# A small memset on GpSimd behind every gather of listed edges

## The chip, the core and the metric

The kernel runs on one core of a Trainium2 chip. Its time is the device time of one execution in microseconds (us). TensorE (PE in the profile, its weight loads PEld), VectorE (DVE), ScalarE (ACT), GpSimd (POOL) and SyncE (SP) each work through an instruction stream of their own, in order, and wait for one another through semaphores.

## What is computed

A graph network with 6250 nodes and 200000 edges: a layer norm with a ReLU, then three layers that take, for every node, the maximum over its incoming edges of the source nodes' rows, and put it through two linear maps. The input is added at the end. The destinations are drawn so that low-numbered nodes have many more edges than high-numbered ones. The widths of a node's row are 128, 256 and 256 on the way into the three layers, and 128 at the end.

```python
def _sage_conv(x, src, dst, Wl, bl, Wr):
    agg = jax.ops.segment_max(x[src], dst, num_segments=x.shape[0])
    agg = jnp.where(jnp.isfinite(agg), agg, 0.0)
    return agg @ Wl + bl + x @ Wr
...
h = jax.nn.leaky_relu(_sage_conv(h, src, dst, Wl1, bl1, Wr1), 0.01)   # and so for layers 2 and 3
...
h = jnp.maximum(_layernorm(x, axis=-1), 0.0)
x = x + _L0_gnn_ref(h, edge_index, ...)
```

## The kernel before

The 6250 nodes lie in 50 tiles of 127 nodes. A first part (to about 270 us in the profile) normalizes the rows and sorts the edges into units. Each unit is a tile of destinations; the edges that fit a regular pattern (one edge for each destination of the unit and each pair of source tiles) are taken by TensorE, the rest stand in lists and are gathered.

**The dense path.** A step is a layer, a group of units (four of them), a pair g of source tiles (25 of them) and a chunk of destinations of up to 512 (layers 1 and 2) or 1024 columns (layer 0). In `one_hots` (L916) a distance product on TensorE goes to PSUM (`sq`, L926, two buffers), and ScalarE turns it into a one-hot matrix (`hot`, L930, eight buffers). In `products` (L934) TensorE multiplies the pair's rows with it (`pg`, L943, two PSUM buffers), and in `maxima` (L948) VectorE takes the maximum with the accumulator `acc` (L955, L957). The loop over steps issues the one-hots of step t between the products of step t-1. There are 200 steps in layer 0 and 350 in each of the layers 1 and 2. SyncE loads the pair of a coming group of steps ahead (`load_pair`, L913, three buffers).

**The listed edges.** The class `Listed` (L959) does the rest. A list has a row of 128 x `len(units)` destinations and a depth for each unit (`CAPS`); one gather fetches, for one unit and one depth, 128 source rows from the layer's table in DRAM with an indirect DMA that GpSimd issues (L980), into a tile `g` of a ring with eight buffers. The indices come as int16 from `ell`; every six (layer 0) or four gathers, ScalarE copies the next ones to an int32 tile `let` (L979, eight buffers). `maximum` (L985 on) merges the tiles on VectorE (L994, L999), and SyncE writes the unit's result to `best` in DRAM (L1003). The depths sum to 145, 291 and 181 in the three lists: 617 gathers in a layer and 1851 in all.

**The finish of a unit.** `Node` (from L1006) fetches the list's result with another indirect DMA of GpSimd (L1025), transposes it on TensorE, merges it with `acc` on VectorE (L1047), runs the linear maps (L1052 to L1060) and writes the new row tables that the next layer gathers from (L1068 on, and L876 to L889). `Joined` does the same for destinations with very many edges (L1095).

**The order.** The scheduler doesn't reorder anything: each engine's stream is in the order of the code. A plan made by hand puts each gather, maximum and finish on a step's agenda (`plan`, `agenda`, `whens`). The gathers of a layer are spread evenly over its steps, ahead of the last of the group's steps that need them, and the maximum follows its gather by 8 steps in layer 0 and 6 in the others. On GpSimd the gathers thus stand in one queue with the fetches (L1025, L1095) and, in the first part and early in layer 0, with the sends of the lists' rows. A send (`send_row`, L599) is a memset of a 128x1 tile `gap_t` (L600) and an indirect DMA that scatters a row of indices to DRAM (L601). In the sends and the gathers alike, GpSimd's DMA_INDIRECT rows in the profile are the time in which it writes the transfer's descriptors, not that of the transfer itself.

A general path (another function) is there for inputs that don't fit the lists; it isn't run for these inputs.

Of the kernel before, what the change touches and what calls it, by code (L numbers as in the profile page):

```python
# [34 lines left out]
BF16 = mybir.dt.bfloat16  # L35
# [6 lines left out]
P = 128  # L42
# [21 lines left out]
def kernel(ctx: ExitStack, tc: tile.TileContext, x, src, dst,  # L64
                    Wl1, bl1, Wr1, Wl2, bl2, Wr2, Wl3, bl3, Wr3, out):
    nc = tc.nc
# [54 lines left out]
    node = main.enter_context(tc.tile_pool(name="node", bufs=1))  # L121
# [771 lines left out]
        nc.vector.memset(hT[:, :, R:], 0.0)  # L893


    RING = 8

    def chunks(layer, k):
# [60 lines left out]
    class Listed:  # L959
# [11 lines left out]
        def gather(self, t):  # L971
            q, j = self.seq[t]
            b, i = divmod(j, self.B)
            if i == 0:
                self.tiles[q, b] = ring.tile([P, self.B, self.F], F32, tag="g", name="g", bufs=RING)
            if j % self.n == 0:
                n = min(self.n, CAPS[self.k][q] - j)
                self.let = ring.tile([P, 6], I32, tag="let", name="let", bufs=8)
                nc.scalar.activation(self.let[:, :n], ell[self.k][:, q, j : j + n], AF.Identity, scale=1.0)  # L979
            nc.gpsimd.indirect_dma_start(  # L980
                out=self.tiles[q, b][:, i, :], out_offset=None, in_=tables[self.layer],
                in_offset=bass.IndirectOffsetOnAxis(ap=self.let[:, j % self.n : j % self.n + 1], axis=0),
            )

        def maximum(self, t):  # L985
            q, j = self.seq[t]
            b, i = divmod(j, self.B)
            m = CAPS[self.k][q]
            if i < self.B - 1 and j < m - 1:
                return  # L990
            base = self.tiles[q, 0]
            if b:
                g = self.tiles.pop((q, b))
                nc.vector.tensor_max(base[:, : i + 1, :], base[:, : i + 1, :], g[:, : i + 1, :])  # L994
            if j == m - 1:
                w = min(m, self.B)
                while w > 1:
                    h = w // 2
                    nc.vector.tensor_max(base[:, :h, :], base[:, :h, :], base[:, w - h : w, :])  # L999
                    w -= h  # L1000
                n = len(LISTS[self.k])
                view = self.to[: n * P, :].rearrange("(p q) f -> p q f", q=n)
                nc.sync.dma_start(view[:, q, :], base[:, 0, :])  # L1003
                del self.tiles[q, 0]
# [587 lines left out]
```

## Time and profile before

| | us |
|---|---|
| median of three runs | 4034.6 (4028.16 to 4065.68) |
| time of the profiled execution | 4023.28 |
| span of the profiled execution | 4021.5 |
| mean granted TensorE clock | 0.854 of full speed |
| busy: TensorE, its weight loads, VectorE, ScalarE, GpSimd | 2844.8, 1818.3, 2433.2, 1477.0, 2214.0 |
| GpSimd: 1851 gathers (L980) | 1868.4 busy |

In rows of groups of instructions, the engine and operation stand first, then the tiles written and read, the shapes and the count; behind the bar the busy time in us, the mean of one instruction in ns, then the idle time of the engine just before such instructions and what ended most of it. In rows of the timeline the start in us and the duration stand first; in brackets stands the engine's idle time before the instruction, with what released it: "issue" is an engine that waited for nothing the profile shows, "remote" a release that it can't place. In rows of stages the stretch is followed by its length, then by busy us and the number of instructions of each engine, the granted clock, the DMA engines' busy share and GB/s; where a row is restricted to a line or a tile, only the engines that it concerns stand in it.

### The profile page before, as it was taken

What the parts mean: (1) busy time and instruction counts of PE and PEld (TensorE: products, weight loads), DVE (VectorE), ACT (ScalarE), POOL (GpSimd) and SP (SyncE); (2) the same over time, 40 slices, a digit from 0 to 9 for tenths busy, and PEclk for the clock granted to TensorE, in tenths of its full rate; (3) what the DMA queues carried; (4) which work ended last, traced back from release to release, by engine and by line L of the source; (5) the groups of instructions that cost most, each with busy time, mean ns of one, the idle gap of its engine ahead of it and who ended that gap; (6) DMA issues with size and microseconds to landing.
All of it is one profiled execution on the core that took longest, in us unless ns stands there. A gap on an engine that the chain in (4) does not pass through costs nothing. (4 is left out here: it accounts for less than half of the span.)

```text
span 4021.5 us, 37441 instructions
## 1 busy us (share of the span) xinstructions
PE 2844.8 (71%) x10999; PEld 1818.3 (45%) x10999; DVE 2433.2 (61%) x3806; ACT 1477.0 (37%) x3139; POOL 2214.0 (55%) x2251
## 2 busy tenths in 40 slices
PE   1044586456644557888888788898888878788787
PEld 1022343233322334555555554565555545455455
DVE  5578576445523344555667677684565667667784
ACT  4322254233322235444433333344444433333233
POOL 5552556665566521566766566631566766567631
PEclk9997687677665679999998898999998988888888
DMA  8111123233322334444545454665344544444545
GB/s 258 38 31 32 40 64 65 72 96 92 91 64 67 102 100 146 121 129 130 121 149 158 149 166 133 198 186 186 110 133 124 121 126 143 123 131 124 175 144 162
DMA packets 261722, 482.67 MB, mean 120 GB/s; under 512 B 54993, under 2 KB 151877, under 8 KB 260867
## 3 DMA queue, kind: packets, MB, share of 16 engines
q0 software_dynamic: 93184, 233.28, 22.3%
q1 hardware_dynamic: 168259, 246.70, 19.0%
q8 instruction: 89, 1.46, 0.2%
q14 instruction: 126, 1.03, 0.1%
q10 hardware_dynamic: 64, 0.20, 0.0%
HBM read 389.65 MB, written 90.31 MB: 119 GB/s over the span
## 5 line engine op out<-in xcount | busy, mean ns | idle before, releaser
L980 POOL DMA_INDIRECT g<-table,let x1851 | 1868.4, 1009 | 1319.8 <-ACT let L979 601.2
L943 PE MATMUL pg<-hot,pair_sb 128*128 128x512 f32 x7000 | 2297.5, 467 | 377.3 <-DVE acc L957 234.7
L957 DVE TENSOR_TENSOR acc<-acc,pg 128x1024 f32<-128x1024 f32 (+3 forms) x1189 | 1379.0, 1172 | 1178.4 <-PE pg L943 447.6
L930 ACT ACTIVATE hot<-sq 128x512 fp32r<-128x512 f32 (+1 forms) x2100 | 1209.6, 590 | 2010.5 <-PE sq L926 1034.8
L943 PEld LDWEIGHTS pg<-hot,pair_sb 128*128 128x128 f32 x7000 | 1420.6, 211 | 970.3 <-issue 372.9
L926 PE MATMUL sq<-lookup,dist 77*128 77x512 bf16 (+1 forms) x1725 | 691.0, 420 | 329.1 <-issue 185.9
L926 PEld LDWEIGHTS <-dist 77*128 77x128 bf16 x2100 | 195.8, 104 | 711.4 <-issue 710.1
L994 DVE TENSOR_TENSOR g<-g 128x1024 f32<-128x1024 f32 (+5 forms) x285 | 297.2, 1043 | 5.4 <-DMA g<-table,let 5.0
L926 PE MATMUL sq<-lookup_o,dist 77*128 77x512 bf16 x375 | 156.6, 433 | 92.6 <-issue 54.1
L1025 POOL DMA_INDIRECT agg<-best,end_i x141 | 137.3, 974 | 99.1 <-PE aT_p L1041 60.7
L999 DVE TENSOR_TENSOR g<-g 128x512 f32<-128x512 f32 (+3 forms) x356 | 177.9, 500 | 10.6
L1054 PE MATMUL z_p<-wr,hT_in 128*128 128x256 f32 (+1 forms) x500 | 143.8, 406 | 0.0
L1060 ACT ACTIVATE s<-z_p,low,slope 128x256 f32<-128x256 f32 x100 | 56.5, 565 | 219.3 <-PE z_p L1056 108.8
L1056 PE MATMUL z_p<-wl,mz 128*128 128x256 f32 (+1 forms) x500 | 125.6, 369 | 1.2 <-DVE mz L1047 1.1
L1054 PEld LDWEIGHTS z_p<-wr,hT_in 128*128 128x128 f32 x500 | 83.2, 209 | 95.2 <-issue 82.0
L1047 DVE TENSOR_TENSOR mz<-acc,aT_p 128x256 f32<-128x256 f32 (+1 forms) x141 | 52.3, 371 | 111.7 <-PE aT_p L1041 46.3
L1095 POOL DMA_INDIRECT agg_v<-best,end_i x24 | 22.7, 948 | 162.4 <-PE vT_p L1104 76.0
L1056 PEld LDWEIGHTS z_p<-wl,mz 128*128 128x128 f32 x500 | 92.8, 211 | 12.9 <-DVE mz L1047 2.0
L1052 PE MATMUL z_p<-bias,ones_b 3*128 3x256 bf16 (+1 forms) x150 | 41.3, 275 | 72.3 <-DVE h L1068 52.5
L979 ACT ACTIVATE let<-ell 128x4 int32<-128x4 int16 (+5 forms) x475 | 92.0, 199 | 0.0
L601 POOL DMA_INDIRECT picks<-picked,to_i x55 | 58.7, 1068 | 38.5 <-DVE rank_h L577 28.7
L885 DVE TENSOR_TENSOR pr<-h,pr 128x256 fp32r<-128x256 f32 x100 | 42.4, 424 | 58.7 <-ACT pr L876 49.1
(281 smaller groups left out, 1195.8 us busy)
## 6 DMA issues: line engine op xcount, KB each, us to landing
pair_sb<-pair SPq DMA_DIRECT2D x200, 512.0 KB
g<-table,let POOLq DMA_INDIRECT x1851
pair_sb<-pair SPq DMA_DIRECT2D x100, 256.0 KB
pair<-pr SPq DMA_DIRECT2D x100, 256.0 KB
best<-g SPq DMA_DIRECT2D x110, 128.0 KB
table<-h SPq DMA_DIRECT2D x100, 128.0 KB
across<-hT SPq DMA_DIRECT2D x100, 128.0 KB
hT_in<-across SPq DMA_DIRECT2D x100, 128.0 KB
```

The source lines that it names most:

```text
L601: s = nc.gpsimd.indirect_dma_start(out=picks[k], out_offset=bass.IndirectOffsetOnAxis(ap=to_i[k][:, i : i + 1], axis=0), in_=picked[k][:, ...
L926: nc.tensor.matmul(d_p[:, :bw], dist[:, 2 * g + s, :], from_[:, base + b : base + b + bw], start=True, stop=True)
L930: nc.scalar.activation(hot[:, :bw], d_p[:, :bw], AF.Relu, bias=1.0, scale=-1.0)
L943: nc.tensor.matmul(to, pr[:, s, i, kk * P : (kk + 1) * P], hot[:, :bw], start=((alone or s == 0) and i == 0), stop=((alone or s == 1) and ...
L957: nc.vector.tensor_max(to, to, of)
L979: nc.scalar.activation(self.let[:, :n], ell[self.k][:, q, j : j + n], AF.Identity, scale=1.0)
L980: nc.gpsimd.indirect_dma_start(out=self.tiles[q, b][:, i, :], out_offset=None, in_=tables[self.layer], in_offset=bass.IndirectOffsetOnAxis ...
L994: nc.vector.tensor_max(base[:, : i + 1, :], base[:, : i + 1, :], g[:, : i + 1, :])
L999: nc.vector.tensor_max(base[:, :h, :], base[:, :h, :], base[:, w - h : w, :])
L1025: nc.gpsimd.indirect_dma_start(out=self.agg[:, : self.F], out_offset=None, in_=of, in_offset=bass.IndirectOffsetOnAxis(ap=at, axis=0),)
L1054: nc.tensor.matmul(z_p, self.hT[:, i, :], wr[layer][:, i, :], start=False, stop=False)
L1056: nc.tensor.matmul(z_p, self.m[:, i, :], wl[layer][:, i, :], start=False, stop=(i == K - 1))
```

## The change

A tile `pace_t` of 128 partitions with 400 bf16 elements each is allocated once, and behind each gather GpSimd fills it with zeros. Nothing else reads or writes the tile.

```diff
+    pace_t = node.tile([P, 400], BF16, name="pace_t")
     RING = 8
...
             nc.gpsimd.indirect_dma_start(
                 out=self.tiles[q, b][:, i, :], out_offset=None, in_=tables[self.layer],
                 in_offset=bass.IndirectOffsetOnAxis(ap=self.let[:, j % self.n : j % self.n + 1], axis=0),
             )
+            nc.gpsimd.memset(pace_t, 0.0)
```

In the built program GpSimd's stream has 1851 more instructions, one behind each L980; 1848 of them wait on GpSimd's own semaphore for the memset before, and none of the gathers has a new wait. The streams of the other engines are the same, instruction by instruction, with the same waits. Lines from L896 on move by one, those behind the gather by two.

## The prediction

> **What bounds the kernel now.** I read the page first (busy shares, slices, groups), then a table of busy times by stage, then the waits, and last the timeline around two chains of GpSimd transfers.
>
> ```profile
> span 4021.5 us, 37441 instructions
> PE 2844.8 (71%) x10999; PEld 1818.3 (45%) x10999; DVE 2433.2 (61%) x3806; ACT 1477.0 (37%) x3139; POOL 2214.0 (55%) x2251
> POOL 5552556665566521566766566631566766567631
> L980 POOL DMA_INDIRECT g<-table,let x1851 | 1868.4, 1009 | 1319.8 <-ACT let L979 601.2
> L930 ACT ACTIVATE hot<-sq 128x512 fp32r<-128x512 f32 (+1 forms) x2100 | 1209.6, 590 | 2010.5 <-PE sq L926 1034.8
> ```
>
> No engine is full over the span. POOL's slices show the gathers of each layer as a plateau of 5 to 7 tenths, with a low slice at the end of each layer. The stages must be read apart. In the next table each row is a stretch: its length, then busy us and instructions of PE, PEld, DVE, ACT and POOL, then TensorE's granted clock. The long rows are the gather phases of layers 0, 1 and 2; the 100 us rows are the ends of the same layers, where nothing is gathered.
>
> ```profile
> 468.00:1450.00 982.00, 545.07 (x1789) 320.89 (x1789) 457.92 (x849) 325.83 (x716) 590.10 (x613) 0.69 0.30 79
> 1500.00:1600.00 100.00, 78.05 (x310) 44.97 (x309) 45.16 (x71) 52.42 (x104) 12.28 (x13) 0.94 0.50 152
> 1663.00:2650.00 987.00, 836.16 (x3330) 549.04 (x3329) 665.18 (x721) 388.33 (x848) 645.45 (x634) 0.92 0.51 150
> 2700.00:2800.00 100.00, 89.89 (x399) 59.11 (x398) 53.82 (x53) 45.60 (x85) 10.42 (x11) 1.00 0.59 197
> 2860.00:3870.00 1010.00, 829.32 (x3321) 539.37 (x3320) 668.09 (x731) 362.83 (x788) 661.45 (x645) 0.89 0.47 134
> 3900.00:4000.00 100.00, 90.46 (x400) 59.27 (x401) 59.59 (x60) 42.21 (x78) 10.41 (x11) 0.98 0.59 183
> ```
>
> Without gathers PE issues 310, 399 and 400 matmuls per 100 us. At those rates the gather phases need 1789/3.10 = 577, 3330/3.99 = 835 and 3321/4.00 = 830 us, and they last 982, 987 and 1010. So 405, 152 and 180 us are lost in them, and no engine's own work explains it. The same view for the gathers' line alone (POOL busy and count):
>
> ```profile
> 468.00:1450.00 982.00, 543.54 (x557) 0.69 0.30 79
> 1663.00:2650.00 987.00, 605.83 (x594) 0.92 0.51 150
> 2860.00:3870.00 1010.00, 619.40 (x602) 0.89 0.47 134
> ```
>
> That is 1753 of the 1851 gathers. The waits tell what is late: first a row for the whole span, then the same wait in the stretch 2700 to 2800 and in 468 to 1450 (us in total, times, longest).
>
> ```profile
> ACT hot L930 <- PE sq L926: 1034.8, 1084, 19.8
> ...
> ACT hot L930 <- PE sq L926: 41.9, 63, 2.1
> ...
> ACT hot L930 <- PE sq L926: 149.7, 135, 19.8
> ```
>
> Without gathers ACT never waits over 2.1 us for a distance product, with them up to 19.8. The timeline shows where: a chain of 20 gathers without a pause, from 468.79 on.
>
> ```profile
> 468.79 0.98 POOL L980 DMA_INDIRECT g<-table,let  x1 [0.31 <-issue]
> 469.89 0.59 PE L926 MATMUL sq<-lookup,dist 77*128 77x512 bf16 x1 [0.85 <-issue]
> 481.16 0.60 ACT L930 ACTIVATE hot<-sq 128x512 fp32r<-128x512 f32 x1 [11.13 <-issue]
> 481.81 0.58 PE L926 MATMUL sq<-lookup,dist 77*128 77x512 bf16 x1 [9.63 <-issue]
> 491.58 0.94 POOL L980 DMA_INDIRECT g<-table,let  x1 [0.31 <-issue]
> 492.83 0.95 POOL L980 DMA_INDIRECT g<-table,let  x1 [0.30 <-issue]
> 495.86 0.60 ACT L930 ACTIVATE hot<-sq 128x512 fp32r<-128x512 f32 x1 [11.30 <-remote]
> ```
>
> The matmul at 469.89 was recorded as done by 470.5, yet ACT, with nothing else to do, starts no one-hot until 481.16, and PE sits 9.63 us behind it. Work flows again once the chain pauses (493.78). I read this as results of PE that reach the other engines late while GpSimd issues transfers back to back; the trace shows the lateness, not its cause. Before the first layer's gathers, GpSimd sends rows (L601) with a 128x1 memset before each. The next rows count the distance matmuls and one-hots there (440 to 452 and 452 to 468), in the bare chain, and in a stage without gathers:
>
> ```profile
> 440.00:452.00 12.00, 4.15 (x12) 6.35 (x12) 0.86 0.05 10
> 452.00:468.00 16.00, 4.05 (x10) 5.14 (x10) 0.80 0.05 9
> 468.00:494.00 26.00, 2.34 (x4) 2.20 (x4) 0.50 0.30 85
> 2700.00:2712.00 12.00, 3.75 (x10) 5.82 (x10) 1.00 0.38 128
> ```
>
> One-hots per us: 1.00, 0.63, 0.15 and 0.83. GpSimd was as busy in the first two as in the third, but its transfers had a memset between them.
>
> **The change part by part.** It adds one tile of 800 bytes per partition, and 1851 memsets on GpSimd, each behind a gather. The streams of PE, DVE, ACT and SP stay as they are; no wait on another engine is added, since nothing else touches the tile and a memset waits only for the memset before it. Queued behind it on GpSimd are the next gather, the fetches of aggregates (L1025) and of the joined list (L1095), and the later row sends.
>
> *Length of one memset.* The tile is 128x400 bf16; the nearest rows are:
>
> ```profile
> masks.py:197 POOL MEMSET ident<- 128x128 f32 x1 | 0.2, 221 | 0.0
> L1576 POOL MEMSET const-bfloat16-1.0<- 128x1 bf16 x1 | 0.1, 114 | 0.0
> ```
>
> 127 more elements cost 107 ns, 0.84 ns each. By elements the new one takes 114 + 399 x 0.84 = 450 ns; by bytes (800 against 512) about 280. I take 0.45 us.
>
> *What of it is hidden.* The chain of sends shows a memset between two transfers:
>
> ```profile
> 441.23 0.19 POOL L600 MEMSET gap_t<- 128x1 f32 x1
> 441.53 0.97 POOL L601 DMA_INDIRECT picks<-picked,to_i  x1
> 442.50 0.11 POOL L600 MEMSET gap_t<- 128x1 f32 x1
> ...
> 199.94 0.54 POOL L600 MEMSET gap_t<- 128x1 f32 x1
> 200.25 1.04 POOL L601 DMA_INDIRECT picks<-picked,to_i  x1
> 201.29 0.11 POOL L600 MEMSET gap_t<- 128x1 f32 x1
> ```
>
> A bare gather has a period of 1.25 us (491.58 to 492.83): 0.95 busy and 0.30 of gap. With a memset the period is 1.27 (441.23 to 442.50), as the memset lies in that gap. One that took 0.54 did not move the start of the next transfer (200.25, again 0.31 after the memset's start); the transfer ended 0.81 after the memset did. So a memset is hidden up to about 1.27 - 0.81 = 0.46 us, and 0.45 just fits. I take +0.025 us each: 557, 594 and 602 of them make 14, 15 and 15 us of POOL, beside 100 outside the windows. Lower end 0, upper end nothing hidden: 0.97 + 0.19 + 0.45 = 1.61, so +0.36 us each, 630 us in all.
>
> *The cover.* POOL's need per phase, transfers busy plus 0.305 us of gap for each of its instructions: 590 + 613 x 0.305 = 777 of 982; 645 + 193 = 838 of 987; 661 + 197 = 858 of 1010. It has 205, 149 and 152 us to spare, 0.37, 0.25 and 0.25 us per gather. The 44 us lie in this room, so they add nothing to the end; if the room were gone, they would be added.
>
> *Blocking by VectorE.* A gather beside a tensor_tensor of VectorE can take longer:
>
> ```profile
> 2108.28 1.22 DVE L994 TENSOR_TENSOR g<-g 128x1024 f32<-128x1024 f32 x1
> 2108.53 1.78 POOL L980 DMA_INDIRECT g<-table,let  x1 [0.30 <-issue]
> ```
>
> The mean gather is 1009 ns against 0.95 undisturbed, about 60 ns. No row has a memset beside such an operation. Between 0 and the same 60 ns again (1753 x 0.06 = 105 us of POOL, still in the room) I take 0, because memset and gather share one gap and a maximum that blocks one has mostly ended when the other starts. The memset could also hold VectorE up; unseen, 0 is taken, and the high end of the range carries it.
>
> The Trainium skill ("SBUF — State Buffer", "Who interferes with whom") says that a VectorE instruction with two SBUF inputs contends with GpSimd only where GpSimd reads SBUF, and infers that tensor_tensor does not starve descriptor generation. By that rule the memset pays 0 under L994, against up to 105 us by the row. The 1.78 us row does not agree with the inference for gathers; whether the first half holds for a memset no run here shows yet.
>
> *What it gives back.* If the memset breaks up the bare chains as it does in the sends, results of PE arrive in time, ACT and PE stop idling, and TensorE's clock (0.69 in layer 0's phase, 0.50 in the bare chain) rises. A phase can't get shorter than POOL's need: 777 + 14 = 791, 853 and 873, so at most 191, 134 and 137 us, 462 in all, can come back (PE's loss of 405, 152 and 180 would allow as much). What is late next: POOL itself, and the lists of indices it waits for (L979 on ACT), so the floor isn't reached. The 452 to 468 row says that relief is partial in long chains (0.63 of a one-hot per us, between 0.15 and 1.00). I take a third, 154 us; ends are a tenth (46) and two thirds (308).
>
> *Sum* against the profiled execution (4023.3 us, span 4021.5): +0 for the memsets, -154: 3869. That execution is 11 us below the median of 4034.6, so the forecast for the median is 3880 us; the likeliest case's own range is 3730 to 3990.
>
> **The rivals.**
>
> *Slower: the memset is not hidden and GpSimd becomes the bound.* If the next gather truly starts its work only when the memset is over, as the end of the row at 200.25 suggests, a longer memset than 0.45 us or a further semaphore wait behind it goes into the period. It decides from 0.25 us per gather in layers 1 and 2 and 0.37 in layer 0, where POOL's room ends. At +0.36 POOL needs 777 + 200 = 977, 838 + 214 = 1052 and 858 + 217 = 1075 us: 0, 65 and 65 over the phases, so +130 even if all idle time is absorbed. POOL's idle time is not all free, since it waits for L979 in ACT's order; with a quarter of the 505 kept idle it is +256 at most. I put it at 4200, range 4080 to 4350. For it: the memset's size is at the edge of the gap, and the size per element comes from one f32 row. Against it: the sends' rows.
>
> *Same: hidden, but no relief.* The lateness may belong to the gathers' data (85 GB/s in the bare chain against 10 in the sends, the last column of those rows) and not to the missing pause; then the memsets vanish in the room and nothing comes back: 4035, range 4000 to 4075. For it: the sends move hardly any data and end before layer 0's gathers. Against it: 2700 to 2712 moves 128 GB/s with one-hots at 0.83 per us.
>
> *The change does not do what it says*, a pause: the memset falls into a gap which is there anyway and the gathers still follow each other at 1.27 us. That is the same case, 4035, and is counted in it.
>
> **How the numbers follow.** The relief has the sends as its one direct witness, and they are not gathers: 0.55. Same: 0.13. Slower: 0.32, as the edge of the gap is narrow and a block by VectorE is unknown. The predicted time is that of the likeliest case, 3880. For 8 in 10, the range runs from 3740 (a part of the largest relief left out) to 4260 (past the slower case's 4200, its tail left out). A measurement of this kernel tells about 1% from no change: faster 0.55, same 0.13, slower 0.32.
>
> **What would show it.** Right: memsets of about 0.45 us or less on POOL between gathers, a period of 1.27 us in unbroken chains, longest waits of ACT for PE well below 19.8 us, clock above 0.69 and a phase shorter than 982 us in layer 0. Wrong on the hiding: periods of 1.5 us or more, POOL's busy tenths at 9 in the gather phases. Wrong on the relief: periods of 1.27, but waits of ten us and more as before. Wrong on VectorE: longer mean times of L994, L999 and L957 than in the profile of before.

## The result, and the profile after

| | before | after |
|---|---|---|
| median of 20 runs each (us) | 4049.07 (4028.16 to 4075.57) | 4068.77 (4051.2 to 4075.05) |
| ratio, 95% interval | | 1.0042 [1.0027, 1.0058] |
| profiled execution: time, span | 4023.28, 4021.5 | 4075.05, 4073.3 |

The change made the kernel slower by 0.4%: 20 us, where the prediction had a gain of 154 as the likeliest. The interval leaves out 1, but so small a step is for practice no change. The profiled execution of before lies at the low end of its runs, so the two traces differ by 52 us, not 20. The lines that answer to those of the prediction, first from the page of after:

```profile
span 4073.3 us, 39291 instructions
PE 2835.9 (70%) x10998; PEld 1823.7 (45%) x10999; DVE 2457.4 (60%) x3806; ACT 1479.0 (36%) x3139; POOL 3053.6 (75%) x4102
POOL 5554788888888812989988888830889888888851
L981 POOL DMA_INDIRECT g<-table,let x1851 | 1873.7, 1012 | 552.4 <-issue 299.7
L985 POOL MEMSET pace_t<- 128x400 bf16 x1851 | 833.1, 450 | 1.0
```

GpSimd's plateau of 5 to 7 tenths has become one of 8 and 9. A memset takes 450 ns. The same stretches as before, from the table of busy times:

```profile
468.00:1450.00 982.00, 555.30 (x1836) 330.07 (x1836) 487.18 (x862) 329.08 (x733) 852.86 (x1177) 0.71 0.30 82
1663.00:2650.00 987.00, 793.89 (x3172) 525.19 (x3172) 636.10 (x689) 372.77 (x808) 880.61 (x1182) 0.92 0.48 143
2860.00:3870.00 1010.00, 799.20 (x3206) 522.83 (x3205) 640.67 (x695) 358.84 (x768) 896.65 (x1208) 0.90 0.45 127
```

In layer 1's stretch POOL is busy for 881 of 987 us, and the pauses of 0.17 us behind its 572 memsets (the timeline below) make another 95: 11 us are left. PE issues fewer matmuls there than before (3172 against 3330). The timeline, in the same part of layer 0 that the prediction showed:

```profile
485.83 1.21 DVE L958 TENSOR_TENSOR acc<-acc,pg 128x1024 f32<-128x1024 f32 x1
486.10 1.09 ACT L931 ACTIVATE hot<-sq 128x512 fp32r<-128x512 f32 x2 [0.29 <-PE sq L927]
486.58 0.45 POOL L985 MEMSET pace_t<- 128x400 bf16 x1
487.06 0.60 PE L927 MATMUL sq<-lookup,dist 77*128 77x512 bf16 x2
487.19 0.95 POOL L981 DMA_INDIRECT g<-table,let  x1 [0.16 <-issue]
487.48 1.09 ACT L931 ACTIVATE hot<-sq 128x512 fp32r<-128x512 f32 x2 [0.29 <-PE sq L927]
488.15 0.45 POOL L985 MEMSET pace_t<- 128x400 bf16 x1
```

Two things are to be seen. A distance product that starts at 487.06 is answered by ACT at 487.48, in the middle of an unbroken chain: the waits of 10 us are gone. And the next gather starts 0.16 us after the memset has *ended* (486.58 + 0.45 = 487.03, then 487.19), so the period is 1.57 us instead of 1.25. The count of distance matmuls and one-hots in the bare chain's stretch (4 and 4 before) says the same:

```profile
468.00:494.00 26.00, 9.34 (x25) 13.50 (x26) 0.76 0.33 96
```

The waits of after and then of before, rows that the prediction didn't need. A wait "for remote" is one for which the trace finds no releaser in time; for ACT's one-hots such waits come with the late results.

```profile
DVE g L996 <- DMA g<-table,let: 268.1, 97, 10.9
PE aT_p L1043 <- DMA agg<-best,end_i: 441.0, 104, 43.7
POOL g L981 <- ACT let L980: 200.3, 29, 63.5
ACT hot L931 <- remote: 6.9, 2, 3.9
```

```profile
ACT hot L930 <- remote: 374.5, 109, 11.8
DVE g L994 <- DMA g<-table,let: 5.0, 4, 2.3
```

What is late now is GpSimd's own work: VectorE waits 268 us for gathered rows (5 before), and TensorE 441 us for the fetched aggregates that stand behind the gathers in GpSimd's queue (6.5 before). GpSimd itself waits for ACT's lists of indices for 200 us in sum (601 before).

Below, "lateness" is a sum taken from a whole trace: for every one-hot before which ACT sat idle for over 0.1 us and that starts over 1 us after its distance matmul, the time from the matmul's start to the one-hot's, less the 0.43 us that it takes undisturbed. It is 1637 us before and 14 us after.

### The profile page after: what moved, and what is told of

Read it like the earlier page. It is cut to its first block, busy times and chain, and to the rows that moved or that the text cites. A ratio compares the mean times of both kernels' runs of the same rounds, so it can differ in the third digit from the quotient of the medians.

```text
span 4073.3 us, 39291 instructions
## 1 busy us (share of the span) xinstructions
PE 2835.9 (70%) x10998; PEld 1823.7 (45%) x10999; DVE 2457.4 (60%) x3806; ACT 1479.0 (36%) x3139; POOL 3053.6 (75%) x4102
## 5 line engine op out<-in xcount | busy, mean ns | idle before, releaser
L981 POOL DMA_INDIRECT g<-table,let x1851 | 1873.7, 1012 | 552.4 <-issue 299.7
L944 PEld LDWEIGHTS pg<-hot,pair_sb 128*128 128x128 f32 x7000 | 1444.2, 214 | 683.5 <-DVE acc L958 392.5
L985 POOL MEMSET pace_t<- 128x400 bf16 x1851 | 833.1, 450 | 1.0
L996 DVE TENSOR_TENSOR g<-g 128x1024 f32<-128x1024 f32 (+5 forms) x285 | 297.9, 1045 | 268.7 <-DMA g<-table,let 268.1
L1043 PE MATMUL aT_p<-ident,agg 128*128 128x128 f32 x250 | 68.6, 344 | 441.9 <-DMA agg<-best,end_i 441.0
L1043 PEld LDWEIGHTS aT_p<-ident,agg 128*128 128x128 f32 x250 | 33.7, 162 | 481.9 <-DMA agg<-best,end_i 258.5
L980 ACT ACTIVATE let<-ell 128x4 int32<-128x4 int16 (+5 forms) x475 | 92.3, 199 | 134.4 <-DMA g<-table,let 133.9
```

The costliest lines, as they stand in the source:

```text
L944: nc.tensor.matmul(to, pr[:, s, i, kk * P : (kk + 1) * P], hot[:, :bw], start=((alone or s == 0) and i == 0), stop=((alone or s == 1) and ...
L981: nc.gpsimd.indirect_dma_start(out=self.tiles[q, b][:, i, :], out_offset=None, in_=tables[self.layer], in_offset=bass.IndirectOffsetOnAxis ...
L985: nc.gpsimd.memset(pace_t, 0.0)
L1043: nc.tensor.transpose(aT_p[:, i, :], self.agg[:, i * P : (i + 1) * P], ident)
```

## The experiments

The theory that came out of the two traces, A: the memset ends the late results, its length goes fully into the gathers' period and makes GpSimd the bound, and the two effects happen to cancel. Then a shorter memset should win. The first runs change one number.

```diff
-    pace_t = node.tile([P, 400], BF16, name="pace_t")
+    pace_t = node.tile([P, 1], BF16, name="pace_t")       # also 100, 200, 300, 800
```

> The tile is 128x1 instead of 128x400. Theory A (two effects that cancel: any memset between gathers ends the late PE results, while the memset's length goes fully into the gather's period and makes GpSimd the bound): memset 0.11 us, period 1.27 us as in the row sends, ACT's wait for a distance product hardly ever late, GpSimd no longer full; 3720 to 3900 us. Rival B (the lateness ends only because of the pause of 0.6 us between two transfers, not because of an instruction in it): period 1.27, ACT still waits 10 to 20 us at worst, 4000 to 4060 us.

> The tile is 128x100. Theory A: memset 0.20 us (0.114 + 99 x 0.84 ns), next gather 0.17 after it, period 1.32 us, no late results; 3740 to 3920 us, 10 to 60 above the 128x1 tile. Rival B: the pause of 0.37 instead of 0.30 us relieves little; 3950 to 4050 us, and below the 128x1 tile.

> The tile is 128x800. Theory A (GpSimd is the bound of the gather phases with 128x400, at 1.565 us per gather): memset 0.785 us, period 1.90 us, some 0.335 us more for each of 1751 gathers: about 590 us more than with 128x400, 4550 to 4700 us. Rival C (the 128x400 version is bound by something else, such as VectorE held up by memsets, and GpSimd's fullness is only a sign): well under that, 4080 to 4350 us.

In the fourth of these runs the memset keeps its 400 elements but stands behind every fourth gather:

```diff
-            nc.gpsimd.memset(pace_t, 0.0)
+            if t % 4 == 3:
+                nc.gpsimd.memset(pace_t, 0.0)
```

> The 128x400 memset stands behind every fourth gather only. Theory A: the mean period is 1.25 + 0.315/4 = 1.33 us, bare chains are four gathers long, for which results were late in 7 to 8 of 100 cases before, so a few waits of 2 to 5 us stay; 3780 to 3930 us. Rival B (each gap between two transfers must be long): lateness about as before, 3980 to 4060 us.

Measured: 3512.19 us for 128x1, 3609.18 for 128x100, 4621.66 for 128x800 (a single run) and 3614.44 behind every fourth. But the kernel before, in the same runs on the same chip, took 3499.42, not 4049. Against that, the 128x1 memset gains nothing (1.0038 [1.0016, 1.0059]), 128x100 loses (1.0314 [1.0297, 1.0331]) and so does every fourth (1.0329 [1.031, 1.0348]). On this chip nothing is late (lateness of 1 us in each of the four traces), and GpSimd is the bound all the same. Layer 0's and layer 1's stretches with 128x1:

```profile
468.00:1450.00 982.00, 666.05 (x2416) 403.13 (x2415) 549.48 (x968) 413.65 (x903) 694.59 (x1215) 0.79 0.40 106
1663.00:2650.00 987.00, 908.36 (x3928) 610.13 (x3927) 748.31 (x817) 458.19 (x973) 703.62 (x1193) 0.98 0.59 176
```

The median period of the gathers is 1.254, 1.317 and 1.896 us with 128x1, 128x100 and 128x800. From 128x100 to 128x800 the time grows by 1012 us for 0.579 us of period: 1749 us per us, which is the number of gathers in the phases (1753). So rival C falls: GpSimd's queue sets the time there, alone from 128x100 on and nearly so below (97 us for 0.063 us from 128x1 to 128x100, 1540 us per us). The runs couldn't tell A from B, since there was no lateness to end. The unchanged kernels came next, with their traces.

> The kernel before, unchanged, to see its trace beside runs of 3499 us as well as beside those of 4049. Theory A2 (the late PE results are a matter of the chip that a run lands on, and were not there in the runs of 3499): where the time is about 3500, the longest waits of ACT for a distance product in the gather phases are a few us and the summed lateness is below 100 us; where it is about 4050, they are 15 to 25 us and some 1600 in sum, as in the first profile. Rival D (lateness is there in every run, and 3499 comes from a faster clock or memory): lateness over 1000 us in sum at 3500 us too.

> The changed kernel, unchanged. Theory A2 with GpSimd as the bound: its gather phases last 1.565 us per gather whichever chip it is, so 3950 to 4080 us, 13 to 16% above before where before takes 3500, and within 1% of it where before takes 4050. Rival D (the chip is faster as a whole by the ratio 3499 to 4049): 3500 to 3550 us beside a before of 3500.

> The 128x1 memset once more. Theory A2: 3480 to 3530 us whichever chip it is, so the same as before where before takes 3500, and 13% faster where before takes 4050, since it ends the lateness and its period stays at 1.25 us. Rival B (only the long pause ends the lateness): about 4050 where before takes 4050.

They landed on another chip, where before took 4067.37 us. Measured: before again 4059.4 (lateness 1672), after 4071.45 (1.0022 [0.9993, 1.005], lateness 59), and the 128x1 memset 4086.16 (1.0047 [1.0005, 1.0089], lateness 1553). So the late results go with the chip that a run lands on (theory A2, first half; rival D, which had lateness at 3500 too, falls with the four traces above, among them the 128x1 kernel, which is late on the one chip and not on the other), and theory A's claim that any memset ends them is wrong: rival B was right about the 128x1 tile. ACT's waits, before again and then with 128x1 on that chip:

```profile
ACT hot L930 <- remote: 417.2, 119, 12.1
```

```profile
ACT hot L931 <- PE sq L927: 973.3, 989, 13.9
ACT hot L931 <- remote: 407.4, 113, 12.0
```

The same program on the two chips has the same chain on GpSimd, first where before takes 3499, then where it takes 4067:

```profile
1001.25 0.12 POOL L985 MEMSET pace_t<- 128x1 bf16 x1
1001.55 0.95 POOL L981 DMA_INDIRECT g<-table,let  x1 [0.19 <-issue]
1002.50 0.12 POOL L985 MEMSET pace_t<- 128x1 bf16 x1
```

```profile
1171.83 0.13 POOL L985 MEMSET pace_t<- 128x1 bf16 x1
1172.14 0.95 POOL L981 DMA_INDIRECT g<-table,let  x1 [0.19 <-issue]
1173.09 0.12 POOL L985 MEMSET pace_t<- 128x1 bf16 x1
```

Next came longer and rarer pauses (128x200; the 128x400 memset behind every second gather, `t % 2 == 1`), and four short memsets on four tiles in place of a long one:

```diff
-    pace_t = node.tile([P, 400], BF16, name="pace_t")
+    pace_t = [node.tile([P, 1], BF16, name=f"pace_t{i}") for i in range(4)]
...
-            nc.gpsimd.memset(pace_t, 0.0)
+            for p_t in pace_t:          # four tiles of 128x1
+                nc.gpsimd.memset(p_t, 0.0)
```

> The tile is 128x200: memset 0.28 us, 0.45 between transfers, period 1.40 us. Theory P (on the chips where before takes 4050, PE results come late as long as GpSimd's pauses between transfers are short; a longer pause ends it, and its price is the longer period): between the 128x1 (lateness some 1550 us in sum) and the 128x400 tile (14 to 59): 200 to 900 us of lateness, 3800 to 3980 us. Where before takes 3500, nothing is late and the period alone counts: 3499 + 1751 x 0.15 = 3760 us. Rival E (a threshold between 0.45 and 0.62 us of pause, below which nothing helps): as before or slower, 4050 to 4150 us, on the first kind of chip.

> The 128x100 memset: period 1.32 us, 0.37 us between transfers. Theory P: where before takes 4050, lateness of 900 to 1500 us and 3920 to 4060 us; where it takes 3500, 3609 again. Rival E: 4050 to 4120 us on the first kind of chip.

> The 128x400 memset behind every second gather: pauses of 0.62 and 0.30 us in turn, mean period 1.41 us. Theory P: where before takes 4050, bare chains are two gathers long, and nothing was late in 92 of 100 cases for chains up to three: lateness below 300 us, 3750 to 3900 us; where before takes 3500, 3765 us. Rival F (each pause has to be long): lateness of 1000 us or more and 4050 us or more on the first kind of chip.

> Four memsets of 128x1 each, on tiles of their own, behind each gather in place of the one of 128x400: the pause between two transfers is about as long, 0.11 x 4 + 0.17 = 0.61 us, but made of short instructions. Theory P (the pause counts): lateness below 150 us and the time of the 128x400 tile within 2% on the same kind of chip (about 4070). Rival G (the long single instruction counts): lateness of 1000 us or more where before takes 4050, and 4300 us or more.

These landed on a third chip, of the kind without lateness (before 3495.43). Measured: 3748.49 (1.0718 [1.0696, 1.074]), 3604.79 (1.0313 [1.0296, 1.033]), 3742.66 (1.0707 [1.0689, 1.0724]) and, in a single run, 3578.3. The expectations of the first three for that kind hold within 23 us; nothing is said on P against E or F. The four short memsets overlapped, and the pause was 0.35 us instead of 0.61:

```profile
603.72 0.20 POOL L986 MEMSET pace_t<- 128x1 bf16 x4
604.07 1.42 POOL L981 DMA_INDIRECT g<-table,let  x1
```

So that run told nothing on pause against instruction (P against G); its time is that of a period of 1.296 us. Three of the kernels were repeated, with the changed one beside them.

> The 128x200 memset once more, for a chip on which before takes 4050. The period alone allows 3750 us (as measured where before takes 3500). Theory P (lateness falls step by step with the pause): 200 to 900 us of lateness in sum, 3800 to 3980 us. Rival E (a threshold between 0.45 and 0.62 us of pause): lateness 1000 us or more, 4050 to 4150 us. Where before takes 3500: 3748 again.

> The 128x400 memset behind every second gather once more, for a chip on which before takes 4050. Theory P: every chain is broken after two gathers by a pause of 0.62 us, lateness below 300 us, 3750 to 3900 us. Rival F (each pause has to be long): lateness of 1000 us or more, 4050 us or more. Where before takes 3500: 3743 again.

> The same behind every fourth gather, for a chip on which before takes 4050. Theory P: lateness 200 to 800 us, 3700 to 3900 us. Rival F: lateness of 1200 us or more, 4030 us or more. Where before takes 3500: 3614 again.

> The changed kernel beside them. Where before takes 4050: 4070 again with hardly any lateness. Where before takes 3500: the line through the 128x100, 128x200 and 128x800 tiles (3609, 3748 and 4622 us at periods of 1.317, 1.400 and 1.896) gives 4040 us at 1.565, 15% slower than before; if the chip as a whole were faster (rival D), 3500 to 3550 us.

Now it was the chip with late results (before 4060.93). Measured: 128x200 3910.99 us (0.9643 [0.9585, 0.9701]), every second 3909.99 (0.9632 [0.9577, 0.9687]), every fourth 3988.85 (0.9846 [0.9779, 0.9914]), after 4071.37 (1.0038 [1.0009, 1.0067]). Lateness: 1152, 1092, 1518 and 47 us. A shorter or rarer pause beats both kernels there, by 3.6% for the first two and by 1.5% for every fourth: it gives up part of the relief for a cheaper period. Theory P's times hold for 128x200 only; its lateness was expected lower for all three (under 900, 300 and 800). Rival E's and F's lateness came true (over 1000), their times didn't. ACT's waits, for 128x200, every second and every fourth:

```profile
ACT hot L931 <- remote: 215.1, 90, 6.5
```

```profile
ACT hot L931 <- remote: 137.7, 71, 5.0
```

```profile
ACT hot L931 <- remote: 310.2, 99, 10.6
```

The last runs fill the curve.

> The tile is 128x300: memset 0.365 us, period 1.48 us. Theory P, with lateness sums of 1553 us at a period of 1.25, 1152 at 1.40 and 14 to 59 at 1.565: 300 to 700 us where before takes 4050, and 3900 to 4000 us, as the period alone allows 3890. Rival E2 (the lateness goes at once between 1.40 and 1.48): below 100 us, 3880 to 3920 us. Where before takes 3500: 3749 + 1751 x 0.083 = 3890 us, no lateness.

> The 128x100 memset, for a chip on which before takes 4050. Theory P: lateness between those of the 128x1 and 128x200 tiles, 1250 to 1500 us, and 3960 to 4060 us. Where before takes 3500: 3607 again.

> The changed kernel. Where before takes 4050: 4070. Where before takes 3500 (not measured yet): 4040 us by the line through the other tiles, 15% slower than before; by rival D (a chip faster as a whole) 3500 to 3550 us.

On the chip with late results (before 4071.41): 128x300 3923.14 us (0.964 [0.9606, 0.9675]), lateness 88; 128x100 4030.79 (0.991 [0.9878, 0.9942]), lateness 1580; after 4069.16 (0.999 [0.9967, 1.0013]), lateness 42. Their waits, 128x100 and then 128x300:

```profile
ACT hot L931 <- remote: 397.0, 110, 11.2
```

```profile
ACT hot L931 <- remote: 14.1, 8, 5.3
DVE g L996 <- DMA g<-table,let: 215.8, 90, 9.8
```

The lateness does not fall step by step: 1553, 1580, 1152, then 88 and 14 to 59 us at periods of 1.254, 1.313, 1.400, 1.482 and 1.566. Rival E2 is right about that (it goes between 1.40 and 1.48), and its time was missed by 3 us. Theory P's times held for both sizes, its lateness for neither. All in one table, with periods as the median distance of two gathers (for every second and fourth the mean, worked out as 1.25 + 0.315/2 and /4):

| memset | period us | time, late results | lateness us | time, none late |
|---|---|---|---|---|
| none (before) | 1.254 | 4049 to 4071 | 1637, 1672 | 3495, 3499 |
| 128x1 | 1.254 | 4086 | 1553 | 3512 |
| 128x100 | 1.313, 1.317 | 4031 | 1580 | 3605, 3609 |
| 128x400, every 4th | 1.33 | 3989 | 1518 | 3614 |
| 128x200 | 1.400 | 3911 | 1152 | 3748 |
| 128x400, every 2nd | 1.41 | 3910 | 1092 | 3743 |
| 128x300 | 1.482 | 3923 | 88 | |
| 128x400 (after) | 1.566 | 4069 to 4071 | 14 to 59 | |
| 128x800 | 1.896 | | | 4622 |

In the last column the time follows the period; by 1749 us per us from 3748, the changed kernel would come to 4039 there, 15% slower than before (not run). In the third column the two curves meet: from 128x300 to 128x400, where nothing is late any more, 146 us for 0.084 us of period are again 1740 us per us. The changed kernel lies some 30 us above GpSimd's line; 17 of them are there before the first gather, which starts at 272.5 us in after and at 255.1 with 128x1 on the chip without lateness. Before lies about 550 us above the line's start at 3499.

## Why the prediction was wrong, point by point

**Where the time was lost before.** Right: TensorE's results came late while GpSimd issued gathers back to back. On a chip without it the same program takes 3499 us, so the lateness cost some 520 to 550 us (the changed kernel, too, is 30 above the line), more than the 462 that the prediction had as the most that could come back. The "same" rival, that the lateness belongs to the gathers' data, fell: with 128x400 the data flows as before (82 against 79 GB/s in layer 0's stretch) and nothing is late, and on the other kind of chip it flows faster (106) with nothing late.

**The length of the memset.** Right: 450 ns forecast, 450 measured; by elements and not by bytes, as was taken.

**What of it is hidden.** This is the step that failed: "a memset is hidden up to about 1.27 - 0.81 = 0.46 us, and 0.45 just fits". Taken was +0.025 us per gather; measured +0.312 (1.566 - 1.254). Both signs that the prediction named for this error are there: periods over 1.5 us, and busy tenths of GpSimd at 9. Next to each other, 128x1, 128x100, 128x200, 128x300 and 128x400 add 0.00, 0.06, 0.15, 0.23 and 0.31 us: from 128x100 on the next gather starts 0.16 or 0.17 us behind the memset's end, and only about the first 0.13 us fit into the old gap of 0.30.

The prediction built a price on the one row of a 0.54 us memset. That was a 128x1 memset, stretched from its usual 0.11 while VectorE ran a TENSOR_SCALAR (in the timeline of before):

```profile
199.70 0.74 DVE L645 TENSOR_SCALAR under<-iota_r,ve 128x1024 f32<-128x1024 f32 x1
```

Its overlap with the next transfer belongs to the tiny tile. Two stretched memsets of 0.39 us show it, from the traces on the chip without lateness, the first of the 128x1 and the second of the 128x100 tile:

```profile
602.60 0.39 POOL L985 MEMSET pace_t<- 128x1 bf16 x1
602.90 0.95 POOL L981 DMA_INDIRECT g<-table,let  x1
```

```profile
470.19 0.39 POOL L985 MEMSET pace_t<- 128x100 bf16 x1
470.74 0.95 POOL L981 DMA_INDIRECT g<-table,let  x1 [0.16 <-issue]
```

Behind the 128x1 memset the next gather starts 0.30 us after the memset's *start*, while it still runs; behind the 128x100 memset it starts 0.16 us after its *end*. All memsets of these two traces that were stretched by over 0.06 us (12 and 11) behave so. So a row of a 128x1 memset, however long it took, was no witness for a tile of 400 elements. Why the size decides, no run shows.

**The cover.** "POOL's room" of 0.37, 0.25 and 0.25 us per gather was worked out rightly, and the break-even points hold: at +0.312 layer 0 gained and the other two lost. From a layer's first gather to the next layer's (to the end for layer 2), the trace has 1359.6, 1206.6 and 1185.0 us before and 1339.1, 1242.9 and 1218.8 after: -20, +36, +34. With the 2 us before the first gather that is the whole difference of the two traces.

**What it gives back.** Mis-sized: a third of 462 was taken, and nearly all of the lateness went (1637 to 14). The witness for it was the wrong one. The row sends have the tiny memset, and a tiny memset ends nothing (lateness 1553); it was the longer memset, with the longer period, that did, and its length was also the price. Neither the relief nor the price was small: the price is 1753 x 0.312 = 547 us, and as the time rose by only 20, the relief was about as much. That the measured 4069 lies among the times the prediction held likely is luck: it lies between two of its cases, and neither had both terms at this size.

**VectorE.** The zero taken was right. The gathers' mean is 1012 ns (1009 before), that of the 128x1024 maxima of L996 is 1222 (1219 before), and the memsets are hardly ever stretched; the tile's row (shortest, median, longest in ns; the count at its end is that of a sample) and two rows of the timeline of after:

```profile
L985 POOL MEMSET pace_t<- x1851: 445/446/658, 274.1 to 3921.6; 128x400 bf16 x186
```

```profile
480.98 1.92 DVE L699 TENSOR_SCALAR acc<-rows_w 128x768 int16<-128x768 int16 x5
481.33 0.55 POOL L985 MEMSET pace_t<- 128x400 bf16 x1
```

Of the memsets that fall beside the two-input maxima of L996, 203 in all, none took over 458 ns. 31 of the 1851 took longer, 24 of them beside a TENSOR_SCALAR (up to 658 beside L699). The Trainium skill ("SBUF — State Buffer", "Who interferes with whom") says that a two-input VectorE instruction contends only with a GpSimd instruction that reads SBUF, and that the two-port modes, for which it names tensor_scalar among others, block the other side. The first agrees with the 203 memsets; the second fits the 24, though no row tells which mode L699 ran in.

**The rivals.** "Slower: GpSimd becomes the bound" had the right mechanism at nearly the right price (0.36 us per gather against 0.312). Its own sum with the measured price, all of GpSimd's idle time absorbed, gives 951, 1023 and 1046 us of need, so -31, +36 and +36: +41 in all, near the +50 of the traces. Its 4200 came out too high by the price and by the idle time that it kept, up to a quarter of what there was. Most of that idle time was the wait for ACT's lists and went with the lateness: GpSimd's wait for `let` fell from 601 to 200 us, and with the 128x1 tile it is 699 us on the chip with late results and 217 on one without. The prediction put relief and price into rival cases, and had no likely case in which two large terms nearly cancel.

## What to carry to other kernels

An instruction put behind a GpSimd transfer is free only as far as the trace shows one of that very size between two transfers; a row in which a tiny one was stretched is no price for a large one. Before a memset is used to space out transfers, work out the break-even per transfer (idle time of the phase over the number of transfers) and try several lengths: here 128x200, 128x300 or every second gather won 3.6% on the chip with late results, where the full length everywhere gained nothing (ratios of 0.999 to 1.0042). And measure on more than one chip: without the late results, 128x200 and every second gather were a loss of 7% (128x300 was not run there).

## What the runs showed of the hardware that was not expected

The same program takes about 550 us less on two of the chips than on a third: before 3495 to 3499 against 4059 to 4071, the 128x1 version 3512 against 4086, with 0.95 us per gather and a period of 1.254 in both traces of the latter. (Before itself was traced only with late results.) The two chips without lateness had one set of runs each, the one with it three; the chip of the first result is not on record, and by its times and its lateness it is of the late kind. The difference lies in when TensorE's results reach ACT and VectorE while GpSimd issues transfers at periods up to 1.40 us; at 1.48 us it is all but gone.

The trace of before narrows the place. In the other direction nothing is late: a distance product that TensorE holds back for ACT starts 0.05 us after the end of the one-hot that it waits for, in the midst of the bare chain too (481.16 + 0.60 = 481.76, then 481.81, in the prediction's rows), and so in all 196 cases in which TensorE sat idle before one. And ACT answers at once: 362 of the 406 late one-hots start within 0.05 us of a recorded event of TensorE's semaphore. So it is that event that comes late, not the answer to it. Whether the product itself or only its message is late stays open, since the profile models the ends of matmuls; so does the reason, and why on that chip only.

Whether it is the pause between the transfers, their rate or the memset that counts is open too, as the four short memsets came out with a shorter pause and on a chip without lateness. A hint for the rate: in the table lateness goes with the mean period, whether each pause is a little longer or a few are much longer (1152 us at 1.400 and 1092 at 1.41; 1580 at 1.313 and 1518 at 1.33).
